# A two-layer transformer on one core: the first cross unit gets its own query buffer, maxima of two units fit into a feed-forward, normalising is written in three groups, and the prologue is put in another order

## The chip, the core and the metric

The kernel runs on one core of a Trainium2 chip. Its engines are TensorE (PE in the profile; PEld is its weight load), VectorE (DVE), ScalarE (ACT), GpSimd (POOL) and SyncE (SP), which issues most of the DMAs. The metric is the device time of one launch in microseconds (us), as the median of several runs.

## The reference

Two layers over `x` of shape (4, 512, 320), with a context of shape (4, 1601, 192), all in float32. Each layer is self-attention, cross-attention and a gated feed-forward, each behind a layer norm and with a residual:

```python
h1 = _ln(x, n1_g, n1_b)
x = _attn(h1, h1, q1, k1, v1, o1_w, o1_b, heads) + x          # 20 heads of 16
h2 = _ln(x, n2_g, n2_b)
x = _attn(h2, context, q2, k2, v2, o2_w, o2_b, heads) + x      # 1601 keys
h3 = _ln(x, n3_g, n3_b)
a, g = jnp.split(h3 @ ff_w1 + ff_b1, 2, axis=-1)               # 2 x 1280
x = a * jax.nn.gelu(g, approximate=False) @ ff_w2 + ff_b2 + x
```

`_attn` projects queries, keys and values, takes a softmax over `q k / 4` and projects the result; `_ln` is `(x - mean) * rsqrt(var + 1e-5) * g + b`.

## The kernel before

The work is cut into units. A unit of attention is one layer, one kind (self or cross), one batch and one group of four heads: five groups a batch, twenty units a kind and layer. They are written `self b g` and `cross b g` below, with b the batch (0 to 3) and g the group (0 to 4). A feed-forward unit is one batch. The order is all self units of a layer, all its cross units, its four feed-forwards, then the next layer.

`main` runs an attention unit over chunks of 128 keys: 4 in a self unit, 13 in a cross unit. For a chunk and a head the scores come as `st` in one PSUM bank (lines 1220): queries and keys are split into a high and a low part, so two products are added. A third (line 1223) subtracts each query's maximum, which lies in a row tile `m`. ACT takes the exponential (line 1233) into a `pr` tile or another place of the same size, and `values` multiplies it with the values into a bank `av` (line 1247), which ACT copies and POOL adds to `o` (line 1264).

The maximum must be known before the scores of its unit, so the scores are computed twice. The maxima of a coming unit are made in `max_pairs`: products `sps` (line 1032), each followed by a DVE reduction over 512 keys (line 1051). A self unit has 16 such reductions, a cross unit 48 and four shorter ones. `giver` hands them out beside the unit that runs: for the next units within two places, and for the first cross unit of a layer (`early`) up to eight units ahead. Where two heads' maxima run beside two heads' scores, or four heads' at once, one round is 8 products and 4 reductions. `max_reduce` and `max_end` turn the result into the `m` rows by a small DMA (line 1105).

Everything else (norms, projections, values, output projections) is put between the chunks by a planner: `add` enters a step into a chain with a cost and a due round, and `steps` picks the most urgent one while its credit lasts. Each step has a condition, such as `unread` in `add_queries`: a unit's queries may be made when the unit that used the same query buffer four attention units before has been scored. There are four query buffers `qbuf`, used in turn. For the `early` unit the due round is the start of the unit two places before.

`add_norm` makes the layer norm of one batch: `stats` (lines 537, 538), `guess_root` and `better_root` (three Newton steps in all, lines 497 to 513) for the root, `normalise` (line 553, DVE, four instructions of 320 columns for a batch, eight in the feed-forward kind), `turn` (transposes on PE at line 566 into `hT`). `turn` also adds the next bias row `brow` to `x` on POOL (line 579).

Before the first unit there is a prologue with `start["on"]` set: no planner, a fixed order of projections, maxima of unit 0 and values. In it `split` (lines 707, 708) and the Newton steps run on DVE; later on POOL. A projection goes through a staging tile `stage` of two buffers, from which DMAs on the SP and ACT queues fill `kT` and `q` (lines 862 and 834).

Of the kernel before, what the change touches and what calls it, by code (L numbers as in the profile page):

```python
# [9 lines left out]
F32 = mybir.dt.float32  # L10
# [3 lines left out]
ALU = mybir.AluOpType  # L14
# [3 lines left out]
B, N, D = 4, 512, 320  # L18
# [5 lines left out]
P = 128  # L24
NQ = N // P
# [101 lines left out]
def kernel(ctx: ExitStack, tc: tile.TileContext, x, context, ws, out):  # L127
# [18 lines left out]
    nc = tc.nc  # L146
    dma = nc.sync.dma_start

    const = ctx.enter_context(tc.tile_pool(name="const", bufs=1))
    wpool = ctx.enter_context(tc.tile_pool(name="weights", bufs=1))  # L150
    one = ctx.enter_context(tc.tile_pool(name="one", bufs=1))
    two = ctx.enter_context(tc.tile_pool(name="two", bufs=2))
    three = ctx.enter_context(tc.tile_pool(name="three", bufs=3))
    dram = ctx.enter_context(tc.tile_pool(name="dram", bufs=1, space=bass.MemoryType.DRAM))
    ps = ctx.enter_context(tc.tile_pool(name="ps", bufs=1, space=PSUM))
    pace_of = Pace()
    see = pace_of.see
# [10 lines left out]
    ident = const.tile([P, P], F32, name="ident")  # L168
    make_identity(nc, ident)

    columns_of = const.tile([P, NC2 * H * VW + SLOT - VW], F32, name="vals")
    nc.gpsimd.memset(columns_of, 1.0)
    vals = columns_of[:, : NC2 * H * VW].rearrange("p (c h w) -> p c h w", h=H, w=VW)
# [6 lines left out]
    for nm in nmax:  # L180
        nc.gpsimd.memset(nm[:, HG * NQ :], 0.0)
    kbuf = [const.tile([P, 4 * QT + P], F32, name=f"kT{i}") for i in range(4)]
    qbuf = [const.tile([P, 2, 2, N // 2], F32, name=f"q{i}") for i in range(4)]

    mrows = [const.tile([P, N], F32, name=f"m{i}") for i in range(2)]
    for m in mrows:
# [4 lines left out]
    see(nc.vector.memset(fill, 1.0))  # L191


    xs = [const.tile([P, NQ, D], F32, name=f"x{b}") for b in range(B)]
    loaded = {}

    def load_x(b):
# [35 lines left out]
    mine = [own[:, i, :] for i in range(7)]  # L233
# [13 lines left out]
    brow = [wpool.tile([P, D], F32, name=f"brow{i}") for i in range(2)]  # L247
# [109 lines left out]
    units = []  # L357
# [7 lines left out]
    at = 0  # L365
# [4 lines left out]
    attn = [u for u in units if u.kind != "ff"]  # L370
    for i, u in enumerate(attn):
        u.n = i
        u.before = attn[i - 1] if i else None

        u.m = (i % (2 * B * G)) % (B * G)
        u.early = u.cross and u.m == 0


        if u.cross:
            u.kT, u.k0 = kbuf[(1, 2, 0, 3)[u.m % 4]], 0  # L380
            u.other = attn[i - (6 if u.m == 1 else 3 if u.m == 2 else 4)] if u.m else None
        else:
            part = u.m % 4 if u.m < B * G - 1 else 0
            u.kT, u.k0 = (kbuf[0], part * N) if part < 3 else (kbuf[2], 0)
            u.other = attn[i - 3] if u.m == B * G - 1 else attn[i - 4] if u.m > 3 or u.m == 3 and u.l else None
        u.qbuf = qbuf[i % 4]
        u.mrow = mrows[i % 2]


# [27 lines left out]
    def add(chain, cost, f, due, ready=yes, soon=yes):  # L417
        chains[chain].append((cost if isinstance(cost, tuple) else (cost,), due, ready, soon, f))
# [15 lines left out]
    def run(chain):  # L434
        costs, _, ready, _, f = chains[chain].popleft()
        assert ready(), chain
        f()
        clock["credit"] -= sum(costs)
# [67 lines left out]
    def better_root(h, y, z):  # L506


        eng = nc.vector if start["on"] else nc.gpsimd
        eng.tensor_tensor(z, y, y, ALU.mult)  # L510
        eng.tensor_tensor(z, z, h, ALU.mult)
        eng.tensor_scalar(z, z, 1.5, None, ALU.add)
        eng.tensor_tensor(y, y, z, ALU.mult)

    hn_used = []
    mvs = [const.tile([P, 6, 2], F32, name=f"mv{i}") for i in range(2)]
    for mv in mvs:
        nc.gpsimd.memset(mv[:, NQ:], 1.0)


    readers = []
# [5 lines left out]
    def add_norm(l, b, i, put, done, due):  # L527
        xb = xs[b]
        s = {}

        def stats(t):
            if t == 0:
                hn_used.append(b)
                mvs.reverse()
                s["mv"] = mvs[0]
            st = three.tile([P, 6], F32, tag="st6", name="st6")
            see(nc.vector.bn_stats(st, xb[:, t, :]))
            see(nc.vector.bn_aggr(s["mv"][:, t, :], st))

        def root(step):  # L540
            if step == 0:
                s["root"] = guess_root(s["mv"][:, :, 1])
                s["rstd"] = [s["root"][1][:, t // 2, t % 2 : t % 2 + 1] for t in range(NQ)]
            for _ in range(step + 1):
                better_root(*s["root"])
            s["round"] = clock["round"]

        def normalise(t):
            if t == 0:
                s["hn"] = one.tile([P, NQ, D + REST], F32, tag="hn", name="hn")  # L550

            for to, at, n in ((0, 0, D), (D, D - REST, REST))[: 1 + i // 2]:
                see(nc.vector.tensor_scalar(  # L553
                    s["hn"][:, t, to : to + n], xb[:, t, at : at + n],
                    s["mv"][:, t, 0:1], s["rstd"][t], ALU.subtract, ALU.mult,
                ))
            s["round"] = clock["round"]

        def turn(k, at, n):
            if k == 0:  # L560
                s["hT"] = two.tile([P, 3, N], F32, tag="hT", name="hT")
                readers.append(done)
            ps = step_bank([P, N], "hps")
            n += REST if n == REST else 0
            for t in range(NQ):
                see(nc.tensor.transpose(ps[:n, t * P : (t + 1) * P], s["hn"][:, t, at : at + n], ident))  # L566
            if start["on"] and k == 1:
                see(nc.vector.tensor_scalar(
                    s["hT"][:n, k, :], ps[:n, :],
                    lng[i][:n, k : k + 1], lnb[i][:n, k : k + 1], ALU.mult, ALU.add,  # L570
                ))
            else:
                see(nc.scalar.activation(
                    s["hT"][:n, k, :], ps[:n, :], AF.Identity,
                    bias=lnb[i][:n, k : k + 1], scale=lng[i][:n, k : k + 1],
                ))
            for t in ((0,), (1,), (2, 3))[k]:

                nc.gpsimd.tensor_tensor(xb[:, t, :], xb[:, t, :], brow[(3 * l + i) % 2], ALU.add)
            if k == 2:  # L580
                hn_used.pop()
                put(s["hT"])

        for t in range(NQ):
            add(
                "norm", LIGHT, lambda t=t: stats(t), due - 22 + t,
                (lambda: stage[b] == 3 * l + i and not hn_used and b in loaded) if t == 0 else yes,
                (lambda: b == 0 or clock["round"] >= loaded[b] + 5) if t == 0 else yes,
            )
        for step in range(2):  # L590
            add(
                "norm", 0.0 if step else LIGHT, lambda step=step: root(step), due - 18 + step, yes,
                (lambda: clock["round"] > s["round"]) if step else yes,
            )
        for t in range(NQ):
            add(
                "norm", LIGHT, lambda t=t: normalise(t), due - 13 + t, yes,
                (lambda: clock["round"] >= s["round"] + 1) if t == 0 else yes,
            )
        for k, at, n in (DK if i < 2 else FK + [(2, 2 * P, REST)]):  # L600
            add(
                "norm", 0.58, lambda k=k, at=at, n=n: turn(k, at, n), due - 6 + 2 * k,
                may_overwrite if k == 0 else yes, lambda: clock["round"] >= s["round"] + 1,
            )
# [124 lines left out]
    def stages(kind="stage"):  # L729
        empty(kind, 1)  # L730
        asked[kind] += 1
        if kind == "kstage":
            kstage.reverse()
            return kstage[0]
        t = two.tile([P, 2, N // 2], F32, tag="stage", name="stage")
        return [t[:, e] for e in range(2)] + [t]

    def slots_soon(us, fs, name, kind="stage"):
# [22 lines left out]
    def add_proj(u):  # L761
# [163 lines left out]

        def unread():

            return u.n < 4 or attn[u.n - 4].scored == attn[u.n - 4].nch

        def free():  # L930

# [2 lines left out]
        def add_queries():  # L934
            if u.g == 0 and u.cross:
                add(chain, 0.0, hold, due - 4, yes, lambda: "h" in u.own)
            for part in range(parts):
                add(chain, (0.05 + 0.427 / parts,) * 3, lambda part=part: queries(part), units[u.i - 2].start if u.early else due - 2, unread)

        if not u.cross:  # L940
            if u.i:
# [514 lines left out]
    def giver(u):  # L1456
# [4 lines left out]
        for v in units[u.i + 1 : u.i + AHEAD + 1]:  # L1461
            if v.kind == "ff":
                break
            coming.append(v)
            if v.i <= u.i + 2 and (v.i == u.i + 1 or u.kind != "ff") or v.early:
                ahead.append(v)
                if v.pairs is None:
                    v.pairs = max_pairs(v)
# [58 lines left out]
    add_proj(units[2])  # L1527
    first = units[0]
    first.pairs = max_pairs(first)
    for chain in ("proj", "proj", "values", None):  # L1530
        round_of([], first.pairs[0].popleft() + first.pairs[1].popleft())
        if chain:
            run(chain)

    run("proj")
    run("values")
    max_reduce(first)
    max_end(first)
    now(load_x(1))
# [5 lines left out]

    for _ in range(4):
        run("values")
    clock["credit"] = 0.0

    for i, u in enumerate(units):  # L1550
# [43 lines left out]
```

## Time and profile before

| What | Value |
| --- | --- |
| median of 3 runs | 2990.22 us (2988.99 to 2995.1) |
| the profiled execution's own time | 2992.5 us |
| its span in the profile | 2990.7 us |
| PE busy | 2922.0 us, 98% |
| DVE busy | 2041.5 us, 68% |
| ACT busy | 1954.5 us, 65% |
| POOL busy | 1326.1 us, 44% |
| mean granted clock of PE | 0.994 |

Busy times are unions of an engine's instructions. In PE up to four matmuls on 32 rows or columns each run side by side and their ends are modelled, so a busy PE is not PE at its peak. The stages can be told by their lines: self units from the first exponential to about 388 us, cross units to about 1247, feed-forwards to about 1530, and layer 1 the same again.

### The profile page before, as it was taken

How to read it: one execution, taken by the hardware profiler on the slowest of the kernel's cores; microseconds unless marked ns; L12 is line 12 of the kernel's file. 1: busy time of each engine (PE TensorE's matmuls, PEld its weight loads, DVE VectorE, ACT ScalarE, POOL GpSimd, SP SyncE). 2: the span in 40 equal slices, each digit the busy share in tenths (PEclk: the TensorE clock that was granted, in tenths of full speed). 3: DMA queues.
4: the chain of work that ended last, by engine and by line, in shares of the span. 5: the costliest groups of instructions: out<-in, count | busy, mean ns of one | idle time of the engine just before them, and what ended most of it. 6: DMA issues, size and time to landing. Idle time of an engine off the chain costs nothing. (4 is left out here: it accounts for less than half of the span.)

```text
span 2990.7 us, 92123 instructions
## 1 busy us (share of the span) xinstructions
PE 2922.0 (98%) x37842; PEld 1608.0 (54%) x37842; DVE 2041.5 (68%) x4011; ACT 1954.5 (65%) x4029; POOL 1326.1 (44%) x1503
## 2 busy tenths in 40 slices
PE   8999999999999999999999999999999999999999
PEld 4455565555555555455554555555555555544555
DVE  6777778878888788422257778778878877873221
ACT  3777577788887888611148775778878878883101
POOL 3556445554555454211125564555554565541100
PEclk8999999999999999999999999999999999999999
DMA  3434221221222121300114332221221221212000
GB/s 104 130 93 114 75 67 46 65 70 36 64 70 52 48 65 28 107 11 0 32 47 102 102 90 68 65 66 31 65 66 37 54 67 39 55 40 71 12 12 14
DMA packets 221150, 178.00 MB, mean 60 GB/s; under 512 B 137652, under 2 KB 175416, under 8 KB 220728
## 3 DMA queue, kind: packets, MB, share of 16 engines
q1 hardware_dynamic: 219928, 171.05, 22.0%
q8 instruction: 297, 4.87, 0.7%
q10 hardware_dynamic: 800, 1.06, 0.1%
q14 instruction: 125, 1.02, 0.1%
HBM read 54.67 MB, written 29.56 MB: 28 GB/s over the span
## 5 line engine op out<-in xcount | busy, mean ns | idle before, releaser
L1051 DVE TENSOR_REDUCE pm<-sps 128x1 f32<-128x512 f32 x1920 | 1190.3, 681 | 108.7 <-PE sps L1032 101.9
L1032 PE MATMUL sps<-kT,q 32*128 32x512 f32 (+1 forms) x6400 | 1061.7, 403 | 17.1 <-DMA q<-stage 7.5
L1233 ACT ACTIVATE pr<-st 128x512 f32<-128x512 f32 (+1 forms) x1710 | 905.6, 603 | 193.7 <-PE st L1223 189.0
L1220 PE MATMUL st<-q,kT 32*128 32x512 f32 (+1 forms) x5440 | 927.4, 433 | 1.9 <-DVE pm L1051 1.5
L1264 POOL TENSOR_TENSOR o<-o,pr 128x512 f32<-128x512 f32 x359 | 461.0, 1284 | 635.2 <-ACT pr L1263 620.4
L1220 PEld LDWEIGHTS st<-q,kT 32*128 32x128 f32 (+1 forms) x5440 | 480.1, 180 | 350.9 <-ACT pr L1233 142.8
L1247 PE MATMUL av<-pr,vals 128*32 128x512 f32 (+1 forms) x3420 | 635.3, 608 | 27.7 <-DVE pm L1051 6.2
L1032 PEld LDWEIGHTS sps<-kT,q 32*128 32x128 f32 x6400 | 549.0, 184 | 117.2 <-DVE pm L1051 22.2
L1223 PE MATMUL st<-m,units 32*128 32x512 f32 (+1 forms) x2720 | 530.4, 391 | 1.7 <-DMA m<-turned 1.7
L1233 ACT ACTIVATE wself<-st 128x512 f32<-128x512 f32 (+1 forms) x867 | 463.3, 604 | 84.5 <-PE st L1223 81.0
L1051 DVE TENSOR_REDUCE nmax<-sps 128x1 f32<-128x512 f32 x640 | 396.6, 681 | 130.9 <-PE sps L1032 124.5
L1247 PE MATMUL av<-wself,vals 128*32 128x512 f32 (+1 forms) x1734 | 369.3, 605 | 9.0 <-DVE pm L1051 3.4
L1264 POOL TENSOR_TENSOR o<-o,wself 128x512 f32<-128x512 f32 x191 | 245.1, 1283 | 297.1 <-ACT wself L1263 296.6
L1342 PE MATMUL fps<-hT,w 128*128 128x512 f32 x640 | 283.4, 596 | 0.0
L1365 ACT ACTIVATE pr<-fps,b 128x512 f32<-128x512 f32 x80 | 54.7, 687 | 348.9 <-PE fps L1355 246.1
L1223 PEld LDWEIGHTS st<-m,units 32*128 32x128 f32 (+1 forms) x2720 | 250.0, 181 | 20.3 <-issue 1.6
L1263 ACT COPY pr<-av 128x512 f32<-128x512 f32 x359 | 220.0, 613 | 18.9 <-PE av L1247 18.5
L1342 PEld LDWEIGHTS fps<-hT,w 128*128 128x128 f32 x640 | 118.9, 190 | 148.6 <-issue 147.5
L1247 PEld LDWEIGHTS av<-pr,vals 128*32 128x32 f32 (+1 forms) x3420 | 91.1, 108 | 195.6 <-DVE pm L1051 104.9
L707 POOL TENSOR_SCALAR stage<-stage 128x256 fp32r<-128x256 f32 (+1 forms) x155 | 106.3, 686 | 146.4 <-ACT stage L857 81.6
L1164 PEld LDWEIGHTS ops<-wo,aT 112*32 112x32 f32 (+1 forms) x3072 | 98.9, 110 | 66.5 <-issue 40.6
L892 PEld LDWEIGHTS kps<-ctxT,w 32*128 32x128 f32 (+1 forms) x4992 | 112.2, 162 | 41.3 <-ACT pr L1233 17.9
(101 smaller groups left out, 3057.0 us busy)
## 6 DMA issues: line engine op xcount, KB each, us to landing
q<-stage SPq DMA_DIRECT2D x157, 256.0 KB
kT<-w SPq DMA_DIRECT2D x120, 208.0 KB
outs<-o SPq DMA_DIRECT2D x80, 256.0 KB
kT<-stage SPq DMA_DIRECT2D x78, 128.0 KB
aT<-outs SPq DMA_DIRECT2D x32, 224.0 KB
oturn<-over SPq DMA_DIRECT2D x32, 224.0 KB
kT<-w SPq DMA_DIRECT2D x40, 144.0 KB
w<-in_L_xattn_ff_w_dram SPq DMA_DIRECT2D x20, 256.0 KB
```

The costliest lines, as they stand in the source:

```text
L707: eng.tensor_scalar(high.bitcast(F32R), x, 1.0, None, ALU.mult)
L892: see(nc.tensor.matmul(ps[to : to + n, :PIECE], lhsT=wk_q[rows, k, u.g * GD : u.g * GD + n], rhs=first.kvT[rows, k, at : at + PIECE], star ...
L1032: see(nc.tensor.matmul(out, lhsT=u.q[rows, t // 2, e, t % 2 * P : (t % 2 + 1) * P].bitcast(F32R), rhs=u.kT[rows, keys].bitcast(F32R), star ...
L1051: see(nc.vector.tensor_reduce(to[:, j : j + 1], ps, AX.X, ALU.max, negate=(ns == 1)))
L1164: see(nc.tensor.matmul(ps[f : f + m, : D // 2], lhsT=aT[:n, k, t * P + f : t * P + f + m], rhs=wo[:n, k, cols], start=(k == 0), stop=(k == 2),
L1220: see(nc.tensor.matmul(st[:r, :], lhsT=keys, rhs=u.q[rows, :, e].bitcast(F32R), start=(e == 0), stop=False))
L1223: see(nc.tensor.matmul(st[:r, :], lhsT=units_of[rows, :r].bitcast(F32R), rhs=u.mrow[rows, :].bitcast(F32R), start=False, stop=True,))
L1233: see(nc.scalar.activation(p[:r], st[:r], AF.Exp))
L1247: see(nc.tensor.matmul(ps[j * SLOT : (j + 1) * SLOT, :], lhsT=columns_of[:r, head : head + SLOT], rhs=pr.pop((c, j))[:r, :], start=True, s ...
L1263: see(nc.scalar.copy(vo, ps))
L1264: nc.gpsimd.tensor_tensor(u.o, u.o, vo, ALU.add)
L1342: see(nc.tensor.matmul(ps, lhsT=w1[:, k, i * FF + c * P : i * FF + (c + 1) * P], rhs=u.hT[:, k, :], start=ahead and k == 0, stop=not ahead ...
```

## The change

Five edits stand together.

1. **Query buffer.** There are five query buffers, and the `early` unit has the fifth. Its `unread` is always true, and its queries are due at the start of the unit four places before it, not two.
2. **Maxima in the feed-forward.** Beside a feed-forward, `giver` now takes the units within two places, if the next unit is a self unit. That is so in the last feed-forward of layer 0 alone.
3. **Normalising.** For self and cross norms outside the prologue, `normalise` writes three groups of 112 columns with a gap of one column between them (target 128 x 3 x 112, step 113), in one instruction of 336 columns. Each `x` tile has 16 more columns, zeroed once, so that the last row can be read that far. The transposes read at the shifted place.
4. **Prologue, order.** Unit 1's queries and keys and two value blocks come ahead of the maxima of unit 0; eight value blocks are done before the first unit, not six. The staging tiles of the prologue are `pr` tiles, each used once. The memsets of `mv` come first on POOL.
5. **Prologue, arithmetic.** A Newton step on DVE ends with one fused instruction in place of two. The `brow` additions for batch 0 come behind the prologue.

```diff
+    mvs = [const.tile([P, 6, 2], F32, name=f"mv{i}") for i in range(2)]
+    for mv in mvs:
+        nc.gpsimd.memset(mv[:, NQ:], 1.0)
...
-    qbuf = [const.tile([P, 2, 2, N // 2], F32, name=f"q{i}") for i in range(4)]
+    qbuf = [const.tile([P, 2, 2, N // 2], F32, name=f"q{i}") for i in range(5)]
...
-    xs = [const.tile([P, NQ, D], F32, name=f"x{b}") for b in range(B)]
+    W3 = 3 * 112
+    xrows = [const.tile([P, NQ * D + W3 - D], F32, name=f"x{b}") for b in range(B)]
+    for xr in xrows:
+        nc.gpsimd.memset(xr[:, NQ * D :], 0.0)
+    xs = [xr[:, : NQ * D].rearrange("p (t d) -> p t d", d=D) for xr in xrows]
...
-        u.qbuf = qbuf[i % 4]
+        u.qbuf = qbuf[4 if u.early else i % 4]
...
+        if start["on"]:
+            eng.scalar_tensor_tensor(y, z, 1.5, y, ALU.add, ALU.mult)
+            return
         eng.tensor_scalar(z, z, 1.5, None, ALU.add)
         eng.tensor_tensor(y, y, z, ALU.mult)
...
+                s["apart"] = i < 2 and not start["on"]
+
+            if i < 2 and not start["on"]:
+                apart = s["hn"][:, t, : 3 * (W3 // 3 + 1)].rearrange("p (k n) -> p k n", k=3)[:, :, : W3 // 3]
+                see(nc.vector.tensor_scalar(
+                    apart, xrows[b][:, t * D : t * D + W3],
+                    s["mv"][:, t, 0:1], s["rstd"][t], ALU.subtract, ALU.mult,
+                ))
+                s["round"] = clock["round"]
+                return
...
-                see(nc.tensor.transpose(ps[:n, t * P : (t + 1) * P], s["hn"][:, t, at : at + n], ident))
+                to = at + (k if s["apart"] else 0)
+                see(nc.tensor.transpose(ps[:n, t * P : (t + 1) * P], s["hn"][:, t, to : to + n], ident))
...
-            for t in ((0,), (1,), (2, 3))[k]:
+            for t in () if start["on"] else ((0,), (1,), (2, 3))[k]:
...
-        t = two.tile([P, 2, N // 2], F32, tag="stage", name="stage")
+        if start["on"]:
+            t = mine[6 - asked[kind]].rearrange("p (e n) -> p e n", e=2)
+        else:
+            t = two.tile([P, 2, N // 2], F32, tag="stage", name="stage")
...
-            return u.n < 4 or attn[u.n - 4].scored == attn[u.n - 4].nch
+            return u.n < 4 or u.early or attn[u.n - 4].scored == attn[u.n - 4].nch
...
-                add(chain, ..., units[u.i - 2].start if u.early else due - 2, unread)
+                add(chain, ..., units[u.i - 4].start if u.early else due - 2, unread)
...
-            if v.i <= u.i + 2 and (v.i == u.i + 1 or u.kind != "ff") or v.early:
+            if v.i <= u.i + 2 and (v.i == u.i + 1 or u.kind != "ff" or units[u.i + 1].kind == "self") or v.early:
...
-    for chain in ("proj", "proj", "values", None):
+    for chain in ("proj", "proj") + ("values",) * 2:
+        run(chain)
+    for chain in (None, "values", "values", None):
         round_of([], first.pairs[0].popleft() + first.pairs[1].popleft())
         if chain:
             run(chain)
 
     run("proj")
-    run("values")
...
+    for t in range(NQ):
+        nc.gpsimd.tensor_tensor(xs[0][:, t, :], xs[0][:, t, :], brow[0], ALU.add)
```

More of the change, by code (lines that the diff above doesn't have):

```diff
@@ L515 @@
     hn_used = []
-    mvs = [const.tile([P, 6, 2], F32, name=f"mv{i}") for i in range(2)]
-    for mv in mvs:
-        nc.gpsimd.memset(mv[:, NQ:], 1.0)
     readers = []
@@ L937, in add_queries @@
             for part in range(parts):
-                add(chain, (0.05 + 0.427 / parts,) * 3, lambda part=part: queries(part), units[u.i - 2].start if u.early else due - 2, unread)
+                add(chain, (0.05 + 0.427 / parts,) * 3, lambda part=part: queries(part), units[u.i - 4].start if u.early else due - 2, unread)
         if not u.cross:
```

## The prediction

> **What bounds the kernel now.** I read the page first: its parts 1 and 2.
>
> ```profile
> span 2990.7 us, 92123 instructions
> ...
> PE 2922.0 (98%) x37842; PEld 1608.0 (54%) x37842; DVE 2041.5 (68%) x4011; ACT 1954.5 (65%) x4029; POOL 1326.1 (44%) x1503
> ```
>
> TensorE (PE) is covered for 98% of the span, so little time is left to take out as plain PE idling. But that busy time is a union over matmuls of which four run side by side, so a PE that waits for a PSUM bank can still look busy. The view of waits tells who makes it wait:
>
> ```profile
> PEld av L1247 <- DVE pm L1051: 173.9, 380, 1.3
> ```
>
> 380 times the weight load of a value product stood until a maximum (line 1051 on VectorE, DVE) gave its bank back: DVE's lateness does reach PE. The third view is the table of stretches, one for each unit, cut where a unit's first exponential (L1233; in the feed-forward the first gelu) starts. The columns are length, then busy time and count of PE, PE's weight loads, DVE, ACT and POOL, then the granted clock:
>
> ```profile
> 322.20:341.00 18.80, 18.32 (x177) 9.09 (x169) 15.80 (x30) 10.89 (x22) 5.71 (x8) 0.85 0.30 82
> 341.00:364.80 23.80, 23.02 (x384) 12.63 (x383) 19.52 (x38) 12.08 (x26) 12.16 (x14) 0.84 0.27 65
> 364.80:388.00 23.20, 22.61 (x370) 14.16 (x372) 20.98 (x49) 12.61 (x30) 7.54 (x7) 1.00 0.14 40
> 1806.70:1822.20 15.50, 14.47 (x215) 7.96 (x207) 11.83 (x23) 11.06 (x25) 6.50 (x9) 1.00 0.36 98
> 1822.20:1846.00 23.80, 23.30 (x395) 13.05 (x394) 23.68 (x46) 12.11 (x26) 11.45 (x11) 1.00 0.27 68
> 1846.00:1868.30 22.30, 21.55 (x385) 14.23 (x388) 18.79 (x45) 12.37 (x29) 9.05 (x10) 1.00 0.15 38
> 1460.50:1530.30 69.80, 69.80 (x396) 36.11 (x396) 23.13 (x47) 10.12 (x18) 7.43 (x19) 1.00 0.07 18
> 1530.30:1551.70 21.40, 20.61 (x231) 9.98 (x224) 20.45 (x37) 11.59 (x24) 5.76 (x6) 1.00 0.22 50
> ```
>
> The first six are the last three self units of layer 0 and of layer 1; then come the last feed-forward of layer 0 and the first self unit of layer 1. An ordinary self unit takes 15.5 us (fourth row, DVE 76%). The units that carry the first cross unit's maxima beside the next one's take 22 to 24 us, with DVE 82, 90, 99 and 84% busy, and the first unit of layer 1 is DVE's too (96%). In the feed-forward DVE is a third busy. So there are places where DVE sets the pace and others, next to them, where it idles.
>
> **The prologue.** These are the timelines of DVE, POOL, PE and SP before the first unit (start, length, engine, line, tiles, count, and the idle time before it with what ended it):
>
> ```profile
> 6.27 0.16 DVE L497 TENSOR_SCALAR root<-mv 128x6 f32<-128x6 f32 x1 [0.46 <-POOL mv L518]
> ...
> 7.25 0.17 DVE L512 TENSOR_SCALAR root<-root 128x6 f32<-128x6 f32 x1
> ...
> 9.27 1.51 DVE L553 TENSOR_SCALAR hn<-x,mv,root 128x320 f32<-128x320 f32 x4
> ...
> 14.04 0.96 DVE L707 TENSOR_SCALAR stage<-stage 128x256 fp32r<-128x256 f32 x1 [1.60 <-ACT stage L857]
> 15.04 0.96 DVE L708 TENSOR_TENSOR stage<-stage 128x256 f32<-128x256 f32 x1
> 17.15 0.53 DVE L707 TENSOR_SCALAR stage<-stage 128x256 fp32r<-128x256 f32 x1 [1.15 <-ACT stage L826]
> ...
> 29.18 0.29 DVE L707 TENSOR_SCALAR stage<-stage 128x256 fp32r<-128x256 f32 x1
> 29.51 0.43 DVE L708 TENSOR_TENSOR stage<-stage 128x256 f32<-128x256 f32 x1
> 29.85 4.87 DVE L1051 TENSOR_REDUCE nmax<-sps 128x1 f32<-128x512 f32 x8
> ```
>
> ```profile
> 6.09 0.14 POOL L518 MEMSET mv<- 128x4 f32 x2
> 13.99 3.54 POOL L579 TENSOR_TENSOR x<-x,brow 128x320 f32<-128x320 f32 x4 [7.76 <-DMA brow<-in_L_xattn_o_b_dram]
> 39.03 0.88 POOL L707 TENSOR_SCALAR stage<-stage 128x256 fp32r<-128x256 f32 x1 [21.50 <-ACT stage L857]
> 39.99 0.72 POOL L708 TENSOR_TENSOR stage<-stage 128x256 f32<-128x256 f32 x1
> 46.73 0.86 POOL L707 TENSOR_SCALAR stage<-stage 128x256 fp32r<-128x256 f32 x1 [6.01 <-ACT stage L826]
> ```
>
> ```profile
> 21.46 1.23 PE L1032 MATMUL sps<-kT,q 32*128 32x512 f32 x8 [6.58 <-DMA q<-stage]
> 22.61 2.79 PE L815 MATMUL qps<-hT,wself 112*32 112x256 f32 x24
> ...
> 28.63 0.74 PE L1032 MATMUL sps<-kT,q 32*128 32x512 f32 x8
> 29.30 0.86 PE L967 MATMUL vps<-wself,hT 112*32 112x128 f32 x24
> ```
>
> Up to the first scores it is one chain. The `mv` memsets move to the front of POOL's list, and DVE no longer waits 0.46 us for them: -0.43. Each of three root steps loses one instruction of 0.17: -0.5. The `brow` additions (13.99 to 17.53) leave; beside them the first splits took 0.96, 0.96 and 0.53, alone the same two forms take 0.29 and 0.43: -0.67 - 0.53 - 0.24 = -1.44. The first score product comes 2.37 us earlier, at 19.1 instead of 21.46.
>
> Behind it the four rounds of the first unit's maxima were spread from 21.46 to 34.72 among projections and splits. In the new order unit 1's queries and keys and two value blocks stand ahead of them, and 16 reductions follow almost bare. One costs 4.87/8 = 0.61, so 1.23 + 16 x 0.61 = 11.0 us instead of 13.26: -2.3. The maxima's way to the `m` rows is the same. Sum -4.7; I take -4.5.
>
> Now PE does the moved work in the gap of 6.58 us before 21.46, which shrinks to about 5.1, since its start moves by 0.93 and its end by 2.37. The two projections and two value blocks take 2 x 1.4 + 2 x 0.86 = 4.5 if a projection of 24 matmuls goes at full speed (half of 2.79). If PE is at half clock there, as at 22.61, all of it doubles to 9.0 and PE is late by 3.9. The two other value blocks that are moved leave the first two units for the wait on the `m` rows; if one of them shortens its unit, that is another -0.8. Hence the ends -5.5 and -0.8. I stay near the first because PE has just run keys and queries back to back.
>
> What costs nothing: the moved `brow` additions (3.54 us) now stand on POOL behind the split that ends at 40.71 and ahead of the one at 46.73, which came after 6.01 us of idling; without that gap, one query split and its DMA would be 3.5 us late, for a unit two ahead. The four memsets of the padded rows run in POOL's idle stretch behind 6.23. The `pr` tiles used as staging are read out long before the exponentials write them. The fifth query buffer adds no instruction. The transposes read one or two columns further on, in the same shape.
>
> **The normalising.** Sixty of the 128 instructions of line 553 (both attention kinds, without batch 0 of layer 0) get the new form:
>
> ```profile
> 60.00:820.00 760.00, 16.74 (x28) 0.99 0.30 77
> 1405.00:2430.00 1025.00, 19.00 (x32) 1.00 0.25 63
> ```
>
> ```profile
> L537 DVE BATCH_NORM_STATS2 st<-x 128x6 f32<-128x320 f32 x96 | 45.1, 470 | 1.8 <-DMA x<-in_x_dram 1.7
> ```
>
> They take 16.74 + 19.00 = 35.7 us, 0.60 each, against 1.51/4 = 0.38 in the prologue with POOL quiet: POOL's long additions hold them up, just as the splits at 14.04. The new form has no row. Its nearest is the statistics instruction, which also walks the same 320 numbers and does not slow down beside POOL: 0.470 x 336/320 = 0.49. Sixty make 29.6, so DVE gains 6.1 us. How much reaches the end depends on PE waiting for DVE; I take 0.6 of it, -3.5. Ends: all, -6.1; and 60 x (0.49 - 0.38) = +6.7 if the new form were both slower and still held up.
>
> The Trainium skill, VectorE: DVE Perf Modes, section "What auto-detection actually checks", says that a one-source operation takes both ports only if the outermost dimensions of source and target are both even or equal; 336 and 3 are neither. SBUF — State Buffer, section "Who interferes with whom", adds that outside the two-port modes an instruction with one SBUF input is not held up by GpSimd. By these rules the end at +6.7 falls away and the sum stays; no row here shows the new form.
>
> **The first cross unit's maxima.** I counted the score products for maxima between the score products of each unit, in the order of both built programs. A round is 8 matmuls (0.74 on PE, row 28.63) and 4 reductions (2.44 on DVE). In layer 0 the last two self units lose 2 and 3 rounds, the second cross unit 1; the four units before get 1, 1, 2 and 0, the first cross unit 2. In layer 1: 3, 2 and 1 against 1, 1, 2, 1 and 1. Twelve leave and twelve arrive. If each leaving one is worth 2.44 in the ten cases in crowded units and 0.74 in two, and each arriving one costs 0.74, the gain is 24.4 + 1.5 - 8.9 = 17 us. If a round costs the same everywhere, it is 0. DVE is the pace for sure only in the units at 90 and 99%, with three leaving rounds each: 6 x (2.44 - 0.74) = 10.2. Such a unit then meets PE's own work, so I take 0.6 of that: -6.
>
> **The feed-forward.** Three rounds of layer 1's second unit go into the feed-forward, one into units 1 to 3; the first unit loses four, 9.8 us of DVE, but cannot fall below an ordinary 15.5: -5.9. PE in the feed-forward is covered without a gap (69.80 of 69.80), so three rounds add 2.2 there and the fourth 0.7. Sum -3. Ends: -5.9, and +2.1 if PE stands for the reductions there (3 x 2.44).
>
> **Sum.** -4.5 - 3.5 - 6 - 3 = -17 on the profiled execution of 2992.5 us (span 2990.7): 2975.5. The median of the three runs is 2990.2, 2.3 below it; so 2973.
>
> **Rivals.** *Only the prologue counts.* PE is covered at 98%, and what DVE is spared elsewhere was hidden, or the new form gains nothing: -4.5, 2986. For it speaks the page's PE line; against it the unit lengths, which follow DVE. 0.2.
>
> *DVE was the whole pace there.* All of 17, with 6.1, 5.9 and 4.5: -33, 2957. Against it, units with DVE at 82 and 84% were as long as those at 99%. 0.14.
>
> *The clock falls* (slower). Rows 322.20 and 341.00 show a granted clock of 0.85 and 0.84, at a unit with six rounds; its sister with five, row 1806.70, kept 1.00 and took 3.3 us less. The change makes eight units with six or seven rounds. If each lost as much, 8 x 3.3 = 26 replaces the -6: -4.5 - 3.5 - 3 + 26 = +15, 3005. It decides from six of the eight, since 6 x 3.3 outweighs 11 by more than the 0.2%. Against it: rows 1822.20 and 1846.00, with nine rounds each, kept 1.00. The Trainium skill, TensorE: Matmul & The Clock Gate, section "Part 1", lets the clock halve after an idle window of about 3.4 us. PE shows no such gap in row 322.20 (18.32 of 18.80), so the trace doesn't bear that out here. 0.1.
>
> **Numbers.** About 0.2% (6 us) is what a measurement here tells from no change. Forecast 0.53, its own range 2963 to 2983; the three rivals have 0.44, and 0.03 is unplaced. Faster: 0.53 + 0.14 + a third of the first rival = 0.74. Same: the rest of that rival and the unplaced, 0.16. Slower: 0.10. The range from 2958 to 2991 takes in the prologue alone and nearly all of the full gain, and leaves out the clock.
>
> **What would show it.** Right: the first score product for maxima at about 19.1 us, the first exponential 4 to 5 us earlier; the new normalising instruction at about 0.5 us, the same with and without POOL beside it; the last self units of both layers at 18 to 20 us; layer 1's first unit near 16, the feed-forward before it about 72. Wrong: normalising above 0.6; the four units before the last ones longer by as much as those got shorter; a clock below 1.00 in them; a feed-forward of 77.

## The result, and the profile after

The changed kernel takes 2972.22 us (median of six runs, 2968.33 to 2974.06); the kernel before, run beside it, takes 2990.47 (2988.99 to 2995.1). The ratio is 0.9933, with a 95% interval of 0.9922 to 0.9944. 2973 was predicted. The profiled execution took 2972.93 us. From the page of the changed kernel:

```profile
span 2971.1 us, 92114 instructions
...
PE 2911.7 (98%) x37842; PEld 1602.1 (54%) x37842; DVE 2037.1 (69%) x4008; ACT 1953.6 (66%) x4029; POOL 1326.7 (45%) x1507
```

The span is 19.6 us shorter, and the busy times hardly differ: DVE, which was to be spared, has 4.4 us less. The gain is in when things happen. The view of waits shows no less of the wait that the prediction began with (173.9 before):

```profile
PEld av L1267 <- DVE pm L1071: 174.9, 381, 1.3
```

The table of stretches, cut at each unit's first exponential as before (length, PE, PE's weight loads, DVE, ACT, POOL, granted clock, share of the DMA engines, GB/s), shows where the time went. In order: the last five self units of layer 0, the last three of layer 1, the last feed-forward of layer 0 and the first self unit of layer 1.

```profile
282.60:299.90 17.30, 16.95 (x268) 9.60 (x264) 13.90 (x28) 11.04 (x22) 6.90 (x8) 1.00 0.26 66
299.90:320.70 20.80, 20.36 (x325) 11.63 (x321) 16.92 (x32) 12.11 (x25) 7.08 (x8) 1.00 0.24 65
320.70:337.80 17.10, 16.76 (x231) 9.47 (x224) 15.81 (x32) 11.37 (x25) 4.36 (x4) 1.00 0.20 58
337.80:355.10 17.30, 17.10 (x370) 9.66 (x362) 15.46 (x31) 11.63 (x26) 11.50 (x11) 1.00 0.37 90
355.10:373.00 17.90, 17.90 (x320) 11.80 (x323) 13.70 (x37) 11.64 (x27) 9.09 (x10) 1.00 0.18 51
1794.30:1811.40 17.10, 16.76 (x231) 9.48 (x224) 15.81 (x32) 11.39 (x25) 4.32 (x4) 1.00 0.20 59
1811.40:1828.70 17.30, 17.10 (x370) 9.63 (x362) 15.46 (x32) 11.63 (x27) 11.53 (x11) 1.00 0.35 82
1828.70:1846.50 17.80, 17.80 (x320) 11.77 (x323) 13.60 (x37) 11.61 (x27) 8.98 (x10) 1.00 0.21 58
1444.00:1516.30 72.30, 72.22 (x415) 36.78 (x411) 29.07 (x55) 10.14 (x18) 7.47 (x19) 1.00 0.07 16
1516.30:1531.70 15.40, 14.54 (x212) 7.65 (x209) 13.30 (x26) 11.21 (x24) 5.29 (x6) 1.00 0.38 87
```

The crowded units went from 22 to 24 us to 17 to 18, the first unit of layer 1 from 21.4 to 15.4, and the feed-forward grew by 2.5. All these rows have a clock of 1.00, where two of before had 0.85 and 0.84. Summed by stage, the difference of the two profiled executions is -5.4 in the prologue, -9.6 in layer 0's self units, -1.5 in its cross units, +2.5 in its feed-forwards, -7.8 in layer 1's self units and +2.2 behind them: -19.6. At half clock were 37.5 us of the execution before (from 17.7, 41.6, 335.2 and 516.1) and 13.7 us of the one after (from 36.4 and 2275.6), so by an estimate up to half of the 23.8 us between them, some 12 of the 19.6, can lie in the clock.

The prologue, in the timelines of DVE, PE and POOL (start, length, engine, line, tiles, count, idle time and what ended it):

```profile
8.09 1.51 DVE L569 TENSOR_SCALAR hn<-x,mv,root 128x320 f32<-128x320 f32 x4
...
12.87 0.29 DVE L724 TENSOR_SCALAR pr<-pr 128x256 fp32r<-128x256 f32 x1 [1.60 <-ACT pr L877]
13.20 0.43 DVE L725 TENSOR_TENSOR pr<-pr 128x256 f32<-128x256 f32 x1
...
19.64 9.66 DVE L1071 TENSOR_REDUCE nmax<-sps 128x1 f32<-128x512 f32 x16 [0.47 <-PE sps L1052]
```

```profile
16.11 1.50 PE L987 MATMUL vps<-wself,hT 112*32 112x128 f32 x48
18.91 0.96 PE L1052 MATMUL sps<-kT,q 32*128 32x512 f32 x10 [1.30 <-DMA q<-pr]
...
35.20 0.49 PE L1243 MATMUL st<-m,units 32*128 32x512 f32 x2 [0.96 <-DMA m<-turned]
```

```profile
35.19 3.34 POOL L1570 TENSOR_TENSOR x<-x,brow 128x320 f32<-128x320 f32 x4
41.31 0.86 POOL L724 TENSOR_SCALAR stage<-stage 128x256 fp32r<-128x256 f32 x1 [2.79 <-ACT stage L846]
```

The first score product starts at 18.91 instead of 21.46, with 1.30 us of PE's old gap of 6.58 left; the splits take 0.29 and 0.43 with POOL quiet; the sixteen reductions run as one block. The first exponential starts at 35.70, 5.4 us earlier. The moved `brow` additions still leave POOL idle for 2.79 us before the next split, so they cost nothing.

The normalising, as the view of one source line gives it (minimum, median and maximum in ns, first and last start, form), first before and then after:

```profile
L553 DVE TENSOR_SCALAR hn<-x,mv,root x128: 301/439/1524, 9.3 to 2910.4; 128x320 f32<-128x320 f32 x96, 128x64 f32<-128x64 f32 x32
```

```profile
L562 DVE TENSOR_SCALAR hn<-x,mv,root x60: 582/614/625, 67.9 to 2283.7; 128x336 f32<-128x336 f32 x60
```

The first line counts all 128 instructions, those of the feed-forward kind and of the prologue too. Of the sixty that get the new form, 32 ran without POOL beside them in the profile before and took 0.40 to 0.44 us; 16 took more than 0.6, and beside each of them POOL was at work for two thirds of the time or more. After, the 17 without POOL take 0.58 to 0.62 us and those with POOL beside them from end to end 0.61 to 0.62. So no instruction is held up any more, but each takes 0.61 us and not 0.49.

### The profile page after: what moved, and what is told of

Read it like the earlier page. It is cut to its first block, busy times and chain, and to the rows that moved or that the text cites. A ratio compares the mean times of both kernels' runs of the same rounds, so it can differ in the third digit from the quotient of the medians.

```text
span 2971.1 us, 92114 instructions
## 1 busy us (share of the span) xinstructions
PE 2911.7 (98%) x37842; PEld 1602.1 (54%) x37842; DVE 2037.1 (69%) x4008; ACT 1953.6 (66%) x4029; POOL 1326.7 (45%) x1507
## 4 chain that ended last, share of the span: by engine, by line
PE 81%; DVE 15%; ACT 1%; issue 1%; POOL 1%; DMA 0%; SPq 0%; ACTq 0%; DVEq 0%; POOLq 0%
PE av L1267 20%; PE st L1240 12%; PE sps L1052 10%; PE fps L1362 9%; DVE pm L1071 8%; PE yps L1417 6%; DVE nmax L1071 4%; PE kps L912 4%; PE ops L1184 4%; PE qps L835 3%; PE vps L1005 3%; PE st L1243 3%; PE fps L1375 2%; PE vps L987 2%; PE kps L869 1%
```

## The experiments

Twelve kernels ran in three sets, the four parts alone on one chip and the other two sets on another. In each set the kernel before ran on the same chip (medians 2991.4, 2990.4 and 2990.0 us). The table has each kernel's median, its ratio to before with the 95% interval, the difference of the medians, and the mean granted clock over its runs; over 65 runs of the kernel before that mean is 0.9944. The ratio is not the quotient of the two medians, so where a difference is within the noise the two can differ in sign.

| Kernel | us | ratio | us to before | clock |
| --- | --- | --- | --- | --- |
| prologue alone | 2987.79 | 0.9989 (0.9981 to 0.9998) | -3.6 | 0.9946 |
| query buffer alone | 2989.80 | 1.0003 (0.9994 to 1.0011) | -1.6 | 0.9952 |
| feed-forward maxima alone | 2994.43 | 1.0017 (1.0007 to 1.0027) | +3.0 | 0.9927 |
| three groups alone | 2990.87 | 1.0004 (0.9995 to 1.0014) | -0.5 | 0.9932 |
| all but three groups | 2976.31 | 0.9950 (0.9937 to 0.9963) | -14.1 | 0.9976 |
| all but feed-forward maxima | 2979.52 | 0.9963 (0.9951 to 0.9975) | -10.9 | 0.9974 |
| all but query buffer | 2981.99 | 0.9969 (0.9959 to 0.9978) | -8.4 | 0.9958 |
| all but prologue | 2978.11 | 0.9958 (0.9946 to 0.9970) | -12.3 | 0.9968 |
| query buffer, own staging | 2986.83 | 0.9986 (0.9976 to 0.9997) | -3.2 | 0.9952 |
| all, own staging | 2969.48 | 0.9927 (0.9915 to 0.9940) | -20.6 | 0.9980 |
| changed kernel again | 2971.48 | 0.9931 (0.9918 to 0.9944) | -18.6 | 0.9980 |
| all, written without gaps | 2979.99 | 0.9959 (0.9944 to 0.9974) | -10.0 | 0.9963 |

**The prologue alone.** Edits 4 and 5 on the kernel before.

```diff
-    for chain in ("proj", "proj", "values", None):
+    for chain in ("proj", "proj") + ("values",) * 2:
+        run(chain)
+    for chain in (None, "values", "values", None):
...
+        if start["on"]:
+            t = mine[6 - asked[kind]].rearrange("p (e n) -> p e n", e=2)
...
+        if start["on"]:
+            eng.scalar_tensor_tensor(y, z, 1.5, y, ALU.add, ALU.mult)
+            return
```

> The prologue's part of the change alone (order of the steps, staging in pr tiles, mv memsets first, fused Newton step, brow additions behind it); query buffer, feed-forward and normalising as before. Theory (the parts add up, each by its own mechanism): first exponential 5.4 us earlier as in the changed kernel, the rest of the run the same, 2984 to 2985 us, that is -5 to -6. Rival (the prologue's gain is given back, since unit 0 is bound by reductions that were only moved): first exponential 5 us earlier, unit 0 and unit 1 together 4 to 5 us longer, within 1.5 us of before.

The first exponential starts 4.7 us earlier and the first unit is 0.8 shorter. Behind it nothing moves by more than 1.5 us in any unit, and 4.7 of the 5.5 are there at the end of the profiled execution. The median falls by 3.6, less than the 5 to 6 expected here. In its steps the part does what was predicted of it.

**The query buffer alone.** Edit 1 on the kernel before.

```diff
-        u.qbuf = qbuf[i % 4]
+        u.qbuf = qbuf[4 if u.early else i % 4]
...
-                add(chain, ..., units[u.i - 2].start if u.early else due - 2, unread)
+                add(chain, ..., units[u.i - 4].start if u.early else due - 2, unread)
```

> The first cross unit's own query buffer alone, due four units ahead. Theory: the reductions leave the crowded last two self units of both layers, -6 to -7 us in each layer's last two units together with +4 to +6 in the four before, and no half clock near 335 us; -7 to -10 us in all, 2980 to 2983. Rival (the clock was the gain): what layer 0 wins beyond layer 1 comes from the clock alone; layer 1, which had full clock before, gains under 1.5 us, and the whole is -3 to -5. Rival (only all parts together free DVE): -2 or less.

The crowded units shorten as in the changed kernel (-6.5 and -5.2 in layer 0, -5.7 and -4.4 in layer 1), and still the kernel gains nothing that its median shows; the profiled execution is 5.0 us shorter. By the median the last of the three expectations is met, but the reason is another one. The largest loss stands in one unit: `self 2 3` of layer 1, 15.2 us before, takes 21.4. Its stretch, and three pieces of 3.4 us from within it:

```profile
1733.20:1754.60 21.40, 17.84 (x229) 9.25 (x227) 11.68 (x20) 13.37 (x28) 15.11 (x18) 0.92 0.40 101
```

```profile
1743.60:1747.00 3.40, 3.22 (x68) 1.94 (x68) 2.04 (x4) 1.99 (x5) 2.59 (x4) 1.00 0.51 110
1747.00:1750.40 3.40, 0.26 (x4) 0.26 (x5) 0.91 (x2) 0.59 (x3) 1.39 (x2) 1.00 0.51 152
1750.40:1753.80 3.40, 3.40 (x20) 1.07 (x23) 1.29 (x2) 2.25 (x5) 1.71 (x4) 0.50 0.17 52
```

The waits of this unit (total us, times, longest) and POOL's timeline in it say why:

```profile
ACT stage L826 <- DMA q<-stage: 4.2, 1, 4.2
...
PE sps L1032 <- ACT stage L826: 3.3, 1, 3.3
```

```profile
1738.32 3.35 POOL L579 TENSOR_TENSOR x<-x,brow 128x320 f32<-128x320 f32 x4
1741.64 0.84 POOL L707 TENSOR_SCALAR stage<-stage 128x256 fp32r<-128x256 f32 x1
```

The early unit's queries now take a place in the staging ring of two buffers here. POOL does its 3.35 us of bias additions before the split, so the DMA out of the staging tile is late; ACT, which wants the tile for the next projection, stands for 4.2 us; PE stands behind ACT for 3.3, and then the clock halves for 3.4. In the changed kernel POOL has the same two steps the other way round:

```profile
1728.58 0.85 POOL L724 TENSOR_SCALAR stage<-stage 128x256 fp32r<-128x256 f32 x1
...
1731.84 3.36 POOL L596 TENSOR_TENSOR x<-x,brow 128x320 f32<-128x320 f32 x4
```

There ACT's wait is 1.4 us and the unit takes 16.3.

**The feed-forward maxima alone.** Edit 2 on the kernel before.

```diff
-            if v.i <= u.i + 2 and (v.i == u.i + 1 or u.kind != "ff") or v.early:
+            if v.i <= u.i + 2 and (v.i == u.i + 1 or u.kind != "ff" or units[u.i + 1].kind == "self") or v.early:
```

> Maxima of two units beside the last feed-forward of layer 0 alone. Theory: that feed-forward 2.5 us longer, layer 1's first unit 6 us shorter, the two after it together about 1 longer: -2.5 us, 2987 to 2988. Rival: the rounds' banks stall the feed-forward, +5 or more there, and nothing is left: 2990 or more.

At its place it does what it does in the changed kernel: +2.5 in the feed-forward, then -6.1, -1.9 and +2.8 in the three units behind it, -2.8 together. Yet the kernel is 3 us slower: the time is the rival's, but the feed-forward is not stalled by 5 us as the rival had it. In the profiled execution the clock halves, among other places, at 1816.9 and at 1823.8, in the crowded units of layer 1 that this edit doesn't touch, and at 1994.4; the mean clock over its runs, 0.9927, is the lowest of all kernels here.

**The three groups alone.** Edit 3 on the kernel before.

```diff
+            if i < 2 and not start["on"]:
+                apart = s["hn"][:, t, : 3 * (W3 // 3 + 1)].rearrange("p (k n) -> p k n", k=3)[:, :, : W3 // 3]
+                see(nc.vector.tensor_scalar(apart, xrows[b][:, t * D : t * D + W3], ..., ALU.subtract, ALU.mult))
```

> Normalising in three groups alone. In the changed kernel the new instruction took 0.61 us on average, at most 0.625, in place of 0.60 on average and up to 1.5. Theory (only DVE's total time counts): 34.6 us in place of 35.7, so within 1.5 us of before, 2989 to 2991. Rival (the prediction's: the long hold-ups are what counts, since PE stands behind them): -3 to -4 us, 2986 to 2988.

No difference that can be measured. The sixty instructions take 34.7 us together, as in the changed kernel (34.6), against 35.7 before.

**All but one.** Since the parts alone come to -2.7 us and the whole to about -18.5, each part was next left out of the changed kernel. What each costs is taken by the differences to before, against the -18.6 of the changed kernel run again. First the normalising:

```diff
-            if i < 2 and not start["on"]:
-                apart = s["hn"][:, t, : 3 * (W3 // 3 + 1)].rearrange("p (k n) -> p k n", k=3)[:, :, : W3 // 3]
```

> The changed kernel without the normalising in three groups. The four parts measured alone came to -3, 0, +5 and 0 us, the whole to -18, so what one part is worth must depend on the others. Theory (normalising is worth nothing in itself: 0.61 us an instruction in place of 0.60): within 2 us of the changed kernel, 2970 to 2975. Rival (it pays once PE is no longer stalled by the crowded units): 3 to 6 us slower than the changed kernel, 2976 to 2978.

4.5 us of the gain go by the medians, though the two intervals (0.9937 to 0.9963, and 0.9918 to 0.9944 for the changed kernel) still overlap. Its profiled execution (2972.3 us) is not longer than that of the changed kernel, and no unit in it is longer by 1 us; the difference is in the other executions, whose clock is 0.997 or 0.998.

The feed-forward maxima:

```diff
-            if v.i <= u.i + 2 and (v.i == u.i + 1 or u.kind != "ff" or units[u.i + 1].kind == "self") or v.early:
+            if v.i <= u.i + 2 and (v.i == u.i + 1 or u.kind != "ff") or v.early:
```

> The changed kernel without the maxima of two units in the feed-forward. Theory (with the query buffer alone, layer 1's unit self 2 3 grew by 6 us, because ACT waited 4.2 us for a staging tile behind POOL's bias additions and PE stood 3.3 us and lost its clock; in the changed kernel the order of layer 1 was another, due to this part): the same stall is back and the 2.6 us of this part are lost, 2978 to 2982. Rival (parts just add up): this part alone was +5, so without it 2967 to 2970.

7.7 us go. The first units of layer 1 lose 6.9 and 4.6 against the changed kernel, with half clock for 3.4 us in each, and the feed-forward gets its 2.5 back. And the staging stall of the query buffer alone is here again in `self 2 3` of layer 1:

```profile
1729.60:1751.30 21.70, 18.29 (x225) 9.64 (x227) 12.00 (x21) 13.36 (x27) 15.52 (x18) 0.87 0.42 104
1743.40:1746.80 3.40, 0.42 (x4) 0.42 (x8) 0.92 (x2) 0.75 (x3) 1.55 (x2) 0.82 0.54 153
1746.80:1750.20 3.40, 3.40 (x24) 0.99 (x27) 1.29 (x2) 2.20 (x5) 1.55 (x4) 0.50 0.21 61
```

POOL has its bias additions ahead of the split again:

```profile
1734.72 3.35 POOL L596 TENSOR_TENSOR x<-x,brow 128x320 f32<-128x320 f32 x4
1738.04 0.84 POOL L724 TENSOR_SCALAR stage<-stage 128x256 fp32r<-128x256 f32 x1
```

So one thing that the second edit does for the first is to shift layer 1's planned steps such that the split comes ahead of the bias additions.

The query buffer:

```diff
-        u.qbuf = qbuf[4 if u.early else i % 4]
+        u.qbuf = qbuf[i % 4]
...
-                add(chain, ..., units[u.i - 4].start if u.early else due - 2, unread)
+                add(chain, ..., units[u.i - 2].start if u.early else due - 2, unread)
```

> The changed kernel without the first cross unit's own query buffer (before's buffer, due two units ahead). Theory: the last self units of both layers are as long as before, with half clock in or near them: 9 to 14 us slower than the changed kernel, 2981 to 2986. Rival (the buffer alone gave nothing, so nothing is lost without it): 2972 to 2975.

10.2 us go. The last two self units are longer than in the changed kernel by 6.5 and 7.9 in layer 0 and by 5.3 and 5.2 in layer 1, with four stretches of half clock in the crowded units:

```profile
331.00:337.80 6.80, 6.72 (x121) 3.99 (x124) 4.14 (x9) 1.50 (x5) 2.79 (x3) 0.50 0.01 4
365.10:371.90 6.80, 6.80 (x74) 3.97 (x75) 3.72 (x12) 2.84 (x7) 1.27 (x1) 0.50 0.03 5
```

The prologue (the reverse of the first experiment's edit):

```diff
-    for chain in ("proj", "proj") + ("values",) * 2:
-        run(chain)
-    for chain in (None, "values", "values", None):
+    for chain in ("proj", "proj", "values", None):
```

> The changed kernel with before's prologue. Theory (the prologue is a stretch by itself): 4 to 6 us slower than the changed kernel, 2976 to 2979. Rival (the prologue also shifts what the planner does in layer 0 or where the half clock falls): off by more than 3 us from that, either way.

6.3 us go: 5.4 at the first exponential, and 2.8 in `self 1 2` of layer 0 with a half clock at 157.4, of which later units give some back.

**Own staging for the early queries.** If the ring of two staging buffers is what cancels the query buffer's gain, a third place for these queries alone should bring it back.

```diff
+    early_stage = w2_flat[:, 3 * D + 4 * kw : 3 * D + 4 * kw + N].rearrange("p (e n) -> p e n", e=2)
...
-                made["q"] = stages()
+                made["q"] = stages("stage", early_stage if u.early else None)
```

> The own query buffer alone, as in the run with that part alone, but the first cross unit's queries are staged in a place of their own (columns of the second feed-forward weight's tile that are free during attention), not in the ring of two staging tiles. Theory (the part alone came to nothing because its queries, moved earlier, waited 4.2 us for a staging tile in layer 1's unit self 2 3): that unit back to 16 to 17 us from 21, 4 to 6 us faster than the part alone, 2984 to 2986. Rival (the wait is only one of several places; the clock falls elsewhere instead): the unit is shorter, the time the same, 2988 to 2991.

`self 2 3` of layer 1 falls back from 21.4 us, at full clock:

```profile
1733.70:1749.90 16.20, 15.84 (x222) 8.77 (x220) 11.51 (x21) 13.21 (x28) 13.81 (x16) 1.00 0.43 109
```

POOL still has its bias additions first (at 1738.82, the split at 1742.14), and no wait for the staging tile of 0.8 us or more is left. So the stall is the staging ring, shown by taking it away. What it is worth in the time is less clear. The median is 3.0 us lower than with the query buffer alone, but that ran on the other chip; against the kernel before of its own set it is -3.2 where the query buffer alone had -1.6, with intervals that overlap, and the unit alone gave 5.1. The median lies between the two expectations. The mean clock is no higher (0.9952); where the executions without a profile lost it is not shown.

**The whole with own staging, and the changed kernel again.** The same edit on the changed kernel, and beside it the changed kernel itself.

> The whole change and the staging place of their own for the first cross unit's queries. Theory: in the changed kernel the staging wait is 1.4 us in layer 1, so there is 0 to 3 us to win, 2969 to 2972. Rival: no staging wait was on the way of PE, within 1 us of the changed kernel.

> The changed kernel once more, on the chip of the other runs of this set, so that they stand beside it: 2971 to 2974, granted clock 0.997 to 0.999.

2969.48 is the lowest median of all, but the two intervals, 0.9915 to 0.9940 and 0.9918 to 0.9944, lie on each other: nothing is to be had there that a measurement can tell. That fits the 1.4 us that the wait has left in the changed kernel.

**The normalising without gaps.** The same 336 columns in one instruction, on the changed kernel, but written as one row without gaps.

```diff
-                apart = s["hn"][:, t, : 3 * (W3 // 3 + 1)].rearrange("p (k n) -> p k n", k=3)[:, :, : W3 // 3]
+                apart = s["hn"][:, t, :W3]
...
-                to = at + (k if s["apart"] else 0)
+                to = at
```

> The changed kernel with the same 336 columns normalised in one instruction, but written without the gaps (target 128 x 336). Theory (the groups take the instruction out of the form that POOL can hold up): alone about 0.45 us, beside POOL's additions up to 1.5 us again, time 2 to 4 us above the changed kernel. Rival (336 columns and the new place of the tile made the difference, not the groups): 0.58 to 0.63 us whatever POOL does, time as the changed kernel.

The view of the source line:

```profile
L562 DVE TENSOR_SCALAR hn<-x,mv,root x60: 415/448/1559, 65.6 to 2285.6; 128x336 f32<-128x336 f32 x60
```

The quick form is quicker at its median (0.45) and held up to 1.56 again; so it is the three groups that end the hold-up, not the width. In the time, the kernel is 8.5 us slower than the changed kernel in the same set, though its sixty instructions take only 2.2 us more (36.75 against 34.56). Where the 8.5 us stand, its profile doesn't show: the profiled execution took 2974.7, none of its units is longer by 2 us, and the executions without a profile go from 2974.4 to 2983.1, at clocks of 0.998 down to 0.995.

## Why the prediction was right

**The prologue (-4.5)** was right in its steps: the score product at 18.91 for 19.1, the splits, the block of reductions (9.66 us for sixteen), the hidden additions. Over the eight profiles with the new prologue the first exponential lies at 36.5 us on the mean (35.7 to 37.4), over the six with the old one at 41.4 (40.8 to 42.5): -4.9. The first unit is 1.4 us shorter besides on the mean, for which the prediction had at most 0.8. By the medians the part is worth 3.6 us alone and 6.3 where it is left out.

**The normalising (-3.5)**: the term was mis-sized at the price of one instruction. The statistics instruction was the wrong neighbour: 0.61 us, not 0.49, so DVE gains 1.2 us (35.74 to 34.56 for the sixty, which overlap a little) and not 6.1. By the prediction's own sign ("above 0.6") this step was wrong, and alone it is worth nothing. Two slips of its arithmetic matter little: 0.6 of 6.1 is 3.7, and 60 x 0.11 is 6.6. That the new form is not held up was right: 582 to 625 ns, beside POOL or not, where the quick form has 415 to 1559. That agrees with the two rules of the Trainium skill cited there (VectorE: DVE Perf Modes, "What auto-detection actually checks", and SBUF — State Buffer, "Who interferes with whom"), and the last experiment shows it for both forms of the target. The form brings 4.5 us in the whole by the medians, and 8.5 against the row without gaps. DVE's total explains 2.2 us of the 8.5 at most; that evenness makes the rest is likely but not shown.

**The first cross unit's maxima (-6)**: the crowded units came to 17.3 to 17.9 us, just under the foreseen 18 to 20. In layer 1, where both executions had full clock, the two last self units lose 11.0 and the five before them gain 8.1 (1.1 to 2.6 each, more than a round's 0.74): -2.9. In layer 0 the last three lose 13.5 and the four before them gain 5.8, -7.7, but 13.7 us of before at half clock lie in these units. Both layers together make -10.6, more than the -6 and with the clock in it; twice layer 1's -2.9, where the clock plays no part, is near -6. So the step was right, and so was its size where the clock plays no part. What it left out is that the moved queries go through the staging ring: alone, the part gives 6.2 us of its gain back there. The prediction had asked what a moved step is moved past, but did that for the prologue and not for the queries.

**The feed-forward (-3)**: +2.5, -6.0, -1.9 and +2.8 at its place, -2.6; foreseen were a feed-forward near 72 (72.3) and a first unit near 16 (15.4). Alone, the kernel is 3.0 us slower with it, at the lowest clock of all.

**The sum.** Adding the four terms was the weak step, and that it held is in part luck. Alone, the parts come to -2.7 us; leaving each out of the whole costs 4.5, 7.7, 10.2 and 6.3, 28.7 together, against a gain of about 18.5. By the ratios in place of the medians the three are +4, 35 and 20.6 us, so the reading is the same. One cause of this is shown, the staging stall, which the first edit brings and the second takes away. The other goes along with the clock. Over the 65 runs of the kernel before, those with a mean clock of 0.997 took 2986.2 us by their median (6 runs), with 0.995 2989.5 (19), with 0.993 2994.0 (13): 2.0 us for 0.001. From 0.9944 to the changed kernel's 0.9980 that is some 7 of the 18.5 us. Stalls and clock can't be parted by it, since a stall of PE can bring the half clock with it, so this is a share that goes along with the clock and not a share caused by it. The profiles, one of each kernel, point the same way: behind the first unit, the five kernels that have edits 1, 2, 4 and 5 together lost the clock in a self unit once between them (own staging, at 1516.5), the other nine 26 times, each at least once.

**The rivals.** *Only the prologue* fell: the units followed DVE. *DVE was the whole pace* fell too: the crowded units stay at 17 to 18 us and don't reach an ordinary 15.5. *The clock falls* was wrong in sign for the whole, whose clock rose; for the feed-forward part alone it is what happened. That the clock could be a gain was no case of the prediction.

**Open.** Why the half clocks fall where they do: the places recur (the prologue and the first unit, `self 1 2` at 155 to 158 us, the crowded units, the first two units of layer 1), but which of them are hit differs in nearly every profile. How the held-up normalising costs 8.5 us without a trace in the profiled execution: its runs have a lower clock (0.9963), which by 2.0 us for 0.001 is some 3.4 of them, and the rest is not placed.

## What to carry to other kernels

Where a schedule is tight, price a moved step with everything that it queues through (here a staging ring of two and the order on POOL), and don't add up parts: run each alone and each left out, since a part worth nothing alone was worth 10 us in the whole. Before reading a difference of a few us, compare the granted clock of the runs. An instruction that always takes the same time can be worth more than one that is mostly quicker and at times held up; here 0.61 us beat a median of 0.45, by a way that the profile didn't show.

## What was not expected of the hardware

The clock falls without a gap that PE's busy time shows. In the kernel before, the stretch ahead of its long half clock has PE covered for 3.21 of 3.40 us, but with only 28 matmuls and DVE busy throughout:

```profile
325.00:328.40 3.40, 3.40 (x49) 2.04 (x44) 2.24 (x7) 2.80 (x7) 1.06 (x1) 1.00 0.74 182
328.40:331.80 3.40, 3.21 (x31) 1.30 (x26) 2.73 (x5) 2.39 (x6) 0.00 (x0) 1.00 0.42 130
331.80:335.20 3.40, 3.21 (x28) 1.69 (x21) 3.40 (x7) 1.52 (x3) 1.27 (x1) 1.00 0.21 74
335.20:338.60 3.40, 3.40 (x19) 1.26 (x15) 3.40 (x7) 1.09 (x2) 0.00 (x0) 0.50 0.01 2
```

The Trainium skill, TensorE: Matmul & The Clock Gate, section "Part 1", has the clock halve after an idle window of about 3.4 us. The stall in the query buffer's experiment bears that out (0.26 of 3.40 us busy, then 0.50); these rows don't, as the busy time reads.

The count of matmuls is the better sign in these units. All half clocks in the fourteen profiles, but for the last of each at its end, last 3.41 us or two, three or four times that. Cut into steps of 3.41 us that fit these, the self units give 2710 stretches at full clock. The clock halves behind 26 of them. In 25 of the 26, and in 26 of the other 2684, 24 matmuls or fewer start; half of all stretches have 48 or more. The busy time doesn't tell the 26 apart: 16 of them read 3.1 us or more of 3.41, and in all 16 DVE is busy for all but 0.04 us or less. So, as far as these traces show, PE can lose its clock beside a DVE full of reductions while it reads as covered; in the case above its weight loads waited for reductions four times between 326 and 337 us, 1.4 us together. The count holds for matmuls of these shapes alone: the last feed-forward starts some 20 in 3.4 us (415 in 72.3) at full clock.
